# Group norm with three neighbouring channels on a partition

## The chip, the cores and the metric

The kernel runs on one NeuronCore of a Trainium2 chip. The metric is device time in microseconds from the first to the last instruction; the number compared is the median over runs. The kernel before took 2606.68 us (median of three runs, 2600.14 to 2608.02). The profiled execution was a run of its own, of 2601.2 us, with a span of 2599.5 us in the trace and a granted TensorE clock of 0.996.

The engines are called as the profile calls them: PE (TensorE, the products), PEld (its weight loads), DVE (VectorE), ACT (ScalarE), POOL (GpSimd), SP (SyncE, which issues most of the transfers).

## What is computed

Eight images of 32 x 32 positions with 384 channels pass through two layers. The first normalizes each image by groups (32 groups of 12 channels, over all positions), applies attention with six heads and relative positions, and adds the input. The second applies layer norm and causal attention over the 1024 positions, adds, and then, for five of the eight images, a feed-forward part with binarized weights and quantized activations. The part that matters here is the group norm, in front of the query, key and value products:

```python
def _gn(v, G=32, eps=1e-5):
    B_, H_, W_, C_ = v.shape
    g = v.reshape(B_, H_, W_, G, C_ // G)
    m = jnp.mean(g, axis=(1, 2, 4), keepdims=True)
    s = jnp.var(g, axis=(1, 2, 4), keepdims=True)
    return ((g - m) / jnp.sqrt(s + eps)).reshape(v.shape)

x = x + _L0_conv_ref(_gn(x), qkv_w, qkv_b, proj_w, proj_b, rel_pos_h, rel_pos_w)
# inside _L0_conv_ref:  qkv = x.reshape(b, hw, c) @ qkv_w + qkv_b
```

The mean and the variance of a group run over 12 neighbouring channels and 1024 positions.

## The kernel before

The kernel holds the image for this step transposed: channels on the 128 partitions, positions along the free dimension, so 384 channels make three blocks of 128 (`NC = 3`). The channel of partition p in block k is 128 k + p. Groups of 12 channels don't fit evenly into blocks of 128, so a group can cross from one block into the next.

```python
NC = C // P                  # 3
GROUPS_GN = 32
CG = C // GROUPS_GN          # 12

def load_T(b):
    xT = pools.image(f"gnT_{b}")
    src = img_T[b].rearrange("(k p) t -> p k t", p=P)
    for k in range(NC):
        nc.sync.dma_start(out=xT[:, k, :], in_=src[:, k, :])
    return xT

def group_norm_T(b, xT=None):
    # ... statistics of each channel: two bn_stats of 512 positions a block, one bn_aggr a block -> mv[:, k, 0:2]
    def over_groups(src, name):                  # channels -> groups, 3 products summed in PSUM
        ps = pools.o_tile(name)
        for k in range(NC):
            nc.tensor.matmul(ps[:GROUPS_GN, 0:1], to_group[:, k, :], src(k), start=(k == 0), stop=(k == NC - 1))
        return ps[:GROUPS_GN, 0:1]

    def to_channels(src, n, name):               # groups -> channels, 3 products
        ps = pools.o_tile(name)
        for k in range(NC):
            nc.tensor.matmul(ps[:, k * n : (k + 1) * n], of_group[:, ts(k, P)], src, start=True, stop=True)
        return ps[:, : NC * n].rearrange("p (k n) -> p k n", k=NC)

    nc.vector.tensor_copy(gm[:, 0:1], over_groups(lambda k: mv[:, k, 0:1], "gmean"))
    mc = to_channels(gm[:, 0:1], 1, "cmean")
    nc.vector.tensor_tensor(d, mv[:, :, 0:1], mc, ALU.subtract)
    nc.vector.tensor_tensor(d, d, d, ALU.mult)
    nc.vector.tensor_tensor(d, d, mv[:, :, 1:2], ALU.add)
    nc.vector.tensor_scalar_add(var, over_groups(lambda k: d[:, k, :], "gvar"), 1e-5)
    nc.scalar.activation(var, var, AF.Sqrt)
    nc.vector.reciprocal(gm[:, 1:2], var)
    nc.vector.tensor_copy(cs, to_channels(gm, 2, "cstat"))
    for k in range(NC):
        nc.vector.tensor_scalar(xT[:, k, :], xT[:, k, :], cs[:, k, 0:1], cs[:, k, 1:2], ALU.subtract, ALU.mult)
    return xT
```

The query and key products (`f_qk` in the profile) contract over the channels, block by block, with weights laid out in the same way (`qkv_w.rearrange("(k p) o -> p k o", p=P)`). They are the first reader of the normalized image.

The order of the stages: image 0 is loaded and normalized first, with nothing before it. Then, for each image b, layer 0 (`layer0`), and the causal attention of layer 1 (`attention1`), in the middle of which the norm of the next image is issued:

```python
for b in range(B):
    xt, more = layer0(b, gn)
    def between():
        return group_norm_T(b + 1) if b + 1 < B else None
    gn = attention1(xt, more, b, between)        # between() is called after the value products (f_v),
    add = ffn(xt, b) if b < B_FFN else None      # before the score products (f_s, L762) and f_av (L776)
```

A framework schedules the instructions of each engine. It puts the small products of the norm between the last `f_v` product and the first few `f_s` products of the attention. The kernel also holds a second path for inputs whose softmax could overflow, which a flag guards.

Of the kernel before, what the change touches and what calls it, by code (L numbers as in the profile page):

```python
# [9 lines left out]
F32 = mybir.dt.float32  # L10
F32R = mybir.dt.float32r
I32 = mybir.dt.int32
AF = mybir.ActivationFunctionType
ALU = mybir.AluOpType
# [3 lines left out]
P = 128  # L18
B, H, W, C = 8, 32, 32, 384
T = H * W  # L20
NJ = T // P
NC = C // P
# [2 lines left out]
FF = 4 * C  # L25
NM = FF // P
GROUPS_GN = 32
CG = C // GROUPS_GN
NG = 5
QB, QEPS = 128.0, 1e-5  # L30
GSB = B // NG
# [43 lines left out]
def conv_attn_hybrid(  # L75
# [19 lines left out]
    nc = tc.nc  # L95
    assert GSB == 1
    const = ctx.enter_context(tc.tile_pool(name="const", bufs=1))
# [20 lines left out]
    def load_weights(pools):  # L118

        nc.scalar.dma_start(out=bqk, in_=qkv_b[0 : 2 * C].rearrange("(m p) -> p m", p=P))  # L120
        rel = pools.page("rel")[:, : 4 * H].rearrange("p (d i) -> p d i", d=2)
        nc.vector.memset(rel, 0.0)
        for half in range(2):
            nc.scalar.dma_start(out=rel[half * HD : (half + 1) * HD, 0, : 2 * H - 1], in_=rel_hT)
            nc.scalar.dma_start(out=rel[half * HD : (half + 1) * HD, 1, : 2 * W - 1], in_=rel_wT)
        nc.scalar.dma_start(out=bv, in_=qkv_b[2 * C : 3 * C].rearrange("(m p) -> p m", p=P))
        nc.scalar.dma_start(out=b1_sb, in_=b1.rearrange("(m p) -> p m", p=P))
        src = qkv_w.rearrange("(k p) o -> p k o", p=P)
        for i in range(3):
            nc.sync.dma_start(out=wqkv_sb[:, :, ts(i, C)], in_=src[:, :, ts(i, C)])  # L130
        nc.sync.dma_start(out=wproj_sb, in_=proj_w.rearrange("(k p) o -> p k o", p=P))
        nc.sync.dma_start(out=pb, in_=proj_b.partition_broadcast(P))
        nc.sync.dma_start(out=wv_sb, in_=wv.rearrange("(k p) o -> p k o", p=P))
        nc.sync.dma_start(out=b2_sb, in_=b2.partition_broadcast(P))

        nc.scalar.mul(wqkv_sb[:, :, 0:C], wqkv_sb[:, :, 0:C], qscale)
        nc.scalar.mul(bqk[:, 0:NPAIR], bqk[:, 0:NPAIR], qscale)
        nc.scalar.mul(rel, rel, 1.0 / qscale)
        nc.scalar.copy(rel_split[:, 0], rel)
        nc.vector.tensor_tensor(rel_split[:, 1], rel, rel_split[:, 0].bitcast(F32), ALU.subtract)  # L140
# [8 lines left out]
        out=maskT, in_=maskT, compare_op=ALU.is_ge, fill=MASKED, base=0, pattern=[[1, P]], channel_multiplier=-1  # L149
# [3 lines left out]
    for i in range(2):  # L153
# [1 line left out]
    ones = const.tile([P, HD], F32, name="ones")  # L155
    nc.gpsimd.memset(ones, 1.0)

    to_group = const.tile([P, NC, GROUPS_GN], F32, name="to_group")
    nc.gpsimd.memset(to_group, 1.0 / CG)
    nc.gpsimd.affine_select(  # L160
        out=to_group, in_=to_group, compare_op=ALU.is_ge, fill=0.0,
        base=0, pattern=[[P, NC], [-CG, GROUPS_GN]], channel_multiplier=1,
    )
    nc.gpsimd.affine_select(
        out=to_group, in_=to_group, compare_op=ALU.is_ge, fill=0.0,
        base=CG - 1, pattern=[[-P, NC], [CG, GROUPS_GN]], channel_multiplier=-1,
    )
    of_group = const.tile([GROUPS_GN, C], F32, name="of_group")
    nc.gpsimd.memset(of_group, 1.0)
    nc.gpsimd.affine_select(  # L170
        out=of_group, in_=of_group, compare_op=ALU.is_ge, fill=0.0,
        base=0, pattern=[[1, C]], channel_multiplier=-CG,
    )
    nc.gpsimd.affine_select(
        out=of_group, in_=of_group, compare_op=ALU.is_ge, fill=0.0,
        base=CG - 1, pattern=[[-1, C]], channel_multiplier=CG,
    )
    unit = const.tile([P, T], F32R, name="unit")

    def make_unit():  # L180
# [112 lines left out]
    def stages(pools):  # L293
# [7 lines left out]
            engine(dst, pt[:, : n * P].rearrange("p (i q) -> p i q", i=n))  # L301

        def load_T(b):
            xT = pools.image(f"gnT_{b}")
            src = img_T[b].rearrange("(k p) t -> p k t", p=P)
            for k in range(NC):
                nc.sync.dma_start(out=xT[:, k, :], in_=src[:, k, :])
            return xT

        def group_norm_T(b, xT=None):  # L310

            xT = load_T(b) if xT is None else xT
            st = pools.small.tile([P, NC, 2, 6], F32, tag="gst", name=f"gst_{b}")
            mv = pools.small.tile([P, NC, 2], F32, tag="gmv", name=f"gmv_{b}")
            for k in range(NC):
                for half in range(2):
                    nc.vector.bn_stats(st[:, k, half, :], xT[:, k, ts(half, 512)])
                nc.vector.bn_aggr(mv[:, k, :], st[:, k, :, :].rearrange("p a s -> p (a s)"))

            def over_groups(src, name):  # L320
                ps = pools.o_tile(name)
                for k in range(NC):
                    nc.tensor.matmul(
                        ps[:GROUPS_GN, 0:1], to_group[:, k, :], src(k), start=(k == 0), stop=(k == NC - 1)
                    )
                return ps[:GROUPS_GN, 0:1]

            def to_channels(src, n, name):
                ps = pools.o_tile(name)
                for k in range(NC):  # L330
                    nc.tensor.matmul(ps[:, k * n : (k + 1) * n], of_group[:, ts(k, P)], src, start=True, stop=True)
                return ps[:, : NC * n].rearrange("p (k n) -> p k n", k=NC)

            gm = pools.small.tile([GROUPS_GN, 2], F32, tag="gm", name=f"gm_{b}")
            nc.vector.tensor_copy(gm[:, 0:1], over_groups(lambda k: mv[:, k, 0:1], "gmean"))
            mc = to_channels(gm[:, 0:1], 1, "cmean")

            d = pools.small.tile([P, NC, 1], F32, tag="gd", name=f"gd_{b}")
            nc.vector.tensor_tensor(d, mv[:, :, 0:1], mc, ALU.subtract)
            nc.vector.tensor_tensor(d, d, d, ALU.mult)  # L340
            nc.vector.tensor_tensor(d, d, mv[:, :, 1:2], ALU.add)
            var = pools.small.tile([GROUPS_GN, 1], F32, tag="gvar", name=f"gvar_{b}")
            nc.vector.tensor_scalar_add(var, over_groups(lambda k: d[:, k, :], "gvar"), 1e-5)
            nc.scalar.activation(var, var, AF.Sqrt)
            nc.vector.reciprocal(gm[:, 1:2], var)
            cs = pools.small.tile([P, NC, 2], F32, tag="gcs", name=f"gcs_{b}")
            nc.vector.tensor_copy(cs, to_channels(gm, 2, "cstat"))
            for k in range(NC):
                nc.vector.tensor_scalar(
                    xT[:, k, :], xT[:, k, :], cs[:, k, 0:1], cs[:, k, 1:2], ALU.subtract, ALU.mult  # L350
                )
            return xT

# [571 lines left out]
        def run(pools):  # L925
            gn = load_T(0)
            if pools.fast:
                load_weights(pools)
            gn = group_norm_T(0, gn)
            if pools.fast:  # L930
                make_unit()
# [25 lines left out]
    with ExitStack() as scope:  # L957
        pools = Pools(scope, tc, "f")
# [43 lines left out]
```

## Time and profile before

| what | value |
|---|---|
| median of three runs | 2606.68 us |
| span of the profiled execution | 2599.5 us |
| PE busy | 2521.0 us, 97% |
| DVE busy | 1619.4 us, 62% |
| ACT busy | 1157.0 us, 45% |
| POOL busy | 115.5 us, 4% |
| gmean and gvar records (128x32 weights, one column) | 48 each, 176 ns mean |
| cmean and cstat records (32x128 weights, one or two columns) | 48 each, 262 ns mean |
| aggregation over 12 numbers (DVE) | 24, 200 ns mean |
| normalization, 128x1024 (DVE) | 24, 809 ns mean |
| load of one block of an image, 512 KB | 24, 4.5 us median to landing |

Busy times overlap, since the engines work side by side. A product of float32 operands leaves two records of PE and two of PEld, so the 48 records of gmean are 24 products: three for each of eight images. Records of PE overlap each other[...]; the distance from start to start says what one costs in a row of products. In a line of the timeline the first number is the start, the second the duration (of all instructions merged in it), and a bracket at the end tells how long the engine was idle before it and which instruction released it. "L762" is a line of the kernel. "out<-in" are the names in the program: `f_s` is a tile of scores, `f_gmean` the PSUM tile of the group means, and so on; the leading "f_" is the fast path.

### The profile page before, as it was taken

The numbers are of one execution on the slowest core, as the hardware profiler recorded it, in microseconds if no ns is written. First come the engines' busy times: TensorE is split into PE (matmuls) and PEld (weight loads), VectorE is DVE, ScalarE is ACT, GpSimd is POOL, SyncE is SP. The second block draws the span as 40 slices with busy tenths as digits, with TensorE's granted clock in tenths as the row PEclk, the third lists the DMA queues.
The fourth block names the chain that finished last, engine by engine and source line by source line (L and its number), as shares of the span: only waits on it lengthen the run. The fifth ranks groups of instructions, "written<-read, shape, count | busy, mean of one in ns | idle before, by whom it ended". The sixth has DMA issues, their size and how long they took to land. (4 is left out here: it accounts for less than half of the span.)

```text
span 2599.5 us, 25162 instructions
## 1 busy us (share of the span) xinstructions
PE 2521.0 (97%) x9538; PEld 1508.4 (58%) x9538; DVE 1619.4 (62%) x2407; ACT 1157.0 (45%) x1513; POOL 115.5 (4%) x106
## 2 busy tenths in 40 slices
PE   7999998999999999999999999999999999999998
PEld 4555685555765556755557555576555555555554
DVE  5895468763587644786545776347864486538652
ACT  4641377421666314764127643156641264127420
POOL 1000002000001000010000100000100010001000
PEclk9999999999999999999999999999999999999999
DMA  6431106011042101150110601003200240015000
GB/s 167 147 146 61 37 1 170 1 61 37 1 117 54 49 13 37 41 130 1 61 37 1 170 1 61 6 31 91 80 25 1 67 104 1 25 39 131 1 1 26
DMA packets 148993, 144.72 MB, mean 56 GB/s; under 512 B 107264, under 2 KB 129664, under 8 KB 147328
## 3 DMA queue, kind: packets, MB, share of 16 engines
q1 hardware_dynamic: 142928, 119.36, 16.4%
q0 software_dynamic: 2880, 23.59, 2.6%
q8 instruction: 77, 1.26, 0.2%
q10 hardware_dynamic: 3056, 0.08, 0.1%
q14 instruction: 52, 0.43, 0.1%
HBM read 75.38 MB, written 42.47 MB: 45 GB/s over the span
## 5 line engine op out<-in xcount | busy, mean ns | idle before, releaser
L558 ACT ACTIVATE f_pr<-f_s 128x1024 f32<-128x1024 f32 x384 | 393.0, 1027 | 403.2 <-PE f_s L554 370.3
L567 DVE TENSOR_TENSOR f_sum<-f_sum,f_pr 128x1024 f32<-128x1024 f32 x288 | 349.0, 1244 | 147.0 <-ACT f_pr L558 145.6
L572 PE MATMUL f_av<-f_pr,f_v 128*64 128x512 f32 x1536 | 359.7, 599 | 0.0
L554 PE MATMUL f_s<-f_q,f_k 128*128 128x512 f32 x768 | 258.5, 418 | 21.8 <-ACT f_pr L558 14.9
L388 PE MATMUL f_qk<-f_gnT,wqkv_sb 128*128 128x512 f32 x576 | 261.5, 598 | 8.2 <-DVE f_k L456 5.6
L554 PE MATMUL f_s<-f_q,f_ks 128*128 128x512 f32 x768 | 245.3, 401 | 0.0
L554 PE MATMUL f_s<-f_r,unit 128*128 128x512 f32 x768 | 243.1, 398 | 0.0
L572 PEld LDWEIGHTS f_av<-f_pr,f_v 128*64 128x64 f32 x1536 | 103.2, 136 | 202.8 <-issue 195.0
L507 DVE TENSOR_TENSOR f_r<-f_near,f_r 32x1024 fp32r<-32x1024 f32 x96 | 193.7, 2017 | 29.0 <-ACT f_r L506 26.3
L554 PEld LDWEIGHTS f_s<-f_q,f_k 128*128 128x128 f32 x768 | 125.8, 189 | 137.9 <-issue 50.3
L762 PE MATMUL f_s<-f_q,f_lnT 128*128 128x512 f32 (+3 forms) x576 | 201.4, 491 | 0.0
L776 PE MATMUL f_av<-f_v,f_pr 128*128 128x385 f32 x576 | 194.5, 486 | 0.0
L388 PEld LDWEIGHTS f_qk<-f_gnT,wqkv_sb 128*128 128x128 f32 x576 | 108.0, 191 | 124.3 <-issue 114.0
L554 PEld LDWEIGHTS f_s<-f_q,f_ks 128*128 128x128 f32 x768 | 145.6, 190 | 35.9
L554 PEld LDWEIGHTS f_s<-f_r,unit 128*128 128x128 f32 x768 | 145.8, 190 | 34.8
L776 PEld LDWEIGHTS f_av<-f_v,f_pr 128*128 128x128 f32 x576 | 108.6, 190 | 78.6 <-issue 11.5
L506 ACT CAST f_r<-f_near 32x1024 fp32r<-32x1024 f32 x96 | 145.9, 1520 | 2.3
L398 PE MATMUL f_v<-wqkv_sb,f_gnT 128*128 128x384 f32 x384 | 129.4, 490 | 10.5 <-ACT f_v L512 8.3
L762 PEld LDWEIGHTS f_s<-f_q,f_lnT 128*128 128x128 f32 x576 | 100.1, 190 | 67.7 <-issue 43.5
L877 DVE TENSOR_REDUCE am<-f_h 128x1 f32<-128x1024 f32 (+2 forms) x80 | 71.6, 946 | 96.6 <-ACT f_h L870 96.6
L770 ACT ACTIVATE f_pr<-f_s 128x1024 f32<-128x1024 f32 (+3 forms) x64 | 41.7, 651 | 202.0 <-DVE f_s L767 202.0
L870 ACT ACTIVATE f_h<-f_y,b_sb 128x256 f32<-128x256 f32 x240 | 100.8, 472 | 67.0 <-PE f_y L866 67.0
(163 smaller groups left out, 3360.6 us busy)
## 6 DMA issues: line engine op xcount, KB each, us to landing
f_far<-f_far SPq DMA_DIRECT2D x48, 512.0 KB, 2.9
f_ks<-f_k SPq DMA_DIRECT2D x96, 256.0 KB, 5.1
f_gnT<-in_xT SPq DMA_DIRECT2D x24, 512.0 KB, 4.5
f_near<-f_far SPq DMA_DIRECT2D x96, 128.0 KB, 3.9
f_x<-in_x SPq DMA_DIRECT2D x32, 384.0 KB, 6.4
out_y<-f_x SPq DMA_DIRECT2D x32, 384.0 KB, 3.8
f_w1a<-w1s POOLq DMA_DIRECT2D x5, 1536.0 KB, 7.2
f_w2a<-w2s POOLq DMA_DIRECT2D x5, 1536.0 KB, 6.6
```

The costliest lines, as they stand in the source:

```text
L388: nc.tensor.matmul(ps[:, half, :], w[:, k, cols], xT[:, k, ts(half, 512)], start=(k == 0), stop=(k == NC - 1),)
L398: nc.tensor.matmul(ps[:, :C], xT[:, k, ts(j, P)], w[:, k, cols], start=(k == 0), stop=(k == NC - 1))
L506: nc.scalar.copy(dst[ts(hi, 32)], src)
L507: nc.vector.tensor_tensor(dst[ts(lo, 32)], src, dst[ts(hi, 32)].bitcast(F32), ALU.subtract)
L554: nc.tensor.matmul(sc[:, half, :], keys[:, ts(c, P)], queries[:, ts(half, 512)], start=(i == 0), stop=(i == 2))
L558: nc.scalar.activation(pr, sc.rearrange("p a n -> p (a n)"), AF.Exp)
L567: nc.vector.tensor_tensor(sums[par], prev, prs[par], ALU.add)
L572: nc.tensor.matmul(avs[half][ts(par, HD), :], v[:, c, ts(h, HD)], prs[par][:, ts(half, 512)], start=(c == 0), stop=(c == NJ - 1),)
L762: nc.tensor.matmul(sc[:, half, lo:], xT[:, c // 4, k, ts(c % 4, P)], q[:, half, k, lo:], start=(k == 0), stop=(k == NC - 1),)
L776: nc.tensor.matmul(av[:, : C + 1], prs[c][:, ts(j - c, P)], v[:, c, :], start=(c == 0), stop=(c == j))
L870: nc.scalar.activation(pairs[i][:, m, :, :], ps[:, ts(i % 2, 256)].rearrange("p (j q) -> p j q", j=2), AF.Identity, bias=b1_sb[:, m : m + 1],)
L877: nc.vector.tensor_reduce(am[:, i, n - 1 : n], pairs[i][:, cuts[n - 1] : cuts[n], :, :], AX.XYZ, ALU.max, apply_absolute_value=True)
```

## The change

The channels are laid out anew: partition p holds the three neighbouring channels 3p, 3p + 1 and 3p + 2. A group of 12 channels is then four whole partitions, and no group crosses a block. The statistics of all three channels of a partition are aggregated together; one product with a 128 x 128 matrix that holds 1/4 where two partitions belong to the same group sums over the group and spreads the sum back to its partitions in one step. A first such product gives the mean, a second the variance. The rows of the query, key and value weights are laid out in the same new order. Its purpose is to have two small products an image in place of twelve, and fewer small vector operations.

The diff, cut to its core:

```diff
-CG = C // GROUPS_GN
+NP_GN = P // GROUPS_GN
...
-        src = qkv_w.rearrange("(k p) o -> p k o", p=P)
+        src = qkv_w.rearrange("(p k) o -> p k o", k=NC)
...
-    to_group = const.tile([P, NC, GROUPS_GN], F32, name="to_group")      # memset, two affine_selects
-    of_group = const.tile([GROUPS_GN, C], F32, name="of_group")          # memset, two affine_selects
+    over_group = const.tile([P, P], F32, name="over_group")
+    nc.gpsimd.memset(over_group, 1.0 / NP_GN)
+    for low in (True, False):
+        nc.gpsimd.affine_select(...)                                     # keeps the blocks of 4 x 4
...
-            src = img_T[b].rearrange("(k p) t -> p k t", p=P)
+            src = img_T[b].rearrange("(p k) t -> p k t", k=NC)
...
-            mv = pools.small.tile([P, NC, 2], F32, tag="gmv", name=f"gmv_{b}")
+            mv = pools.small.tile([P, 2], F32, tag="gmv", name=f"gmv_{b}")
             for k in range(NC):
                 for half in range(2):
                     nc.vector.bn_stats(st[:, k, half, :], xT[:, k, ts(half, 512)])
-                nc.vector.bn_aggr(mv[:, k, :], st[:, k, :, :].rearrange("p a s -> p (a s)"))
-            ... over_groups and to_channels, gmean, cmean, gvar, cstat: 12 products, as shown above
+            nc.vector.bn_aggr(mv, st.rearrange("p k a s -> p (k a s)"))
+
+            ps = pools.o_tile(f"gmean_{b}")
+            nc.tensor.matmul(ps[:, 0:1], over_group, mv[:, 0:1], start=True, stop=True)
+            cs = pools.small.tile([P, 2], F32, tag="gcs", name=f"gcs_{b}")
+            nc.vector.tensor_copy(cs[:, 0:1], ps[:, 0:1])
+            d = pools.small.tile([P, 2], F32, tag="gd", name=f"gd_{b}")
+            nc.vector.tensor_tensor(d[:, 0:1], mv[:, 0:1], cs[:, 0:1], ALU.subtract)
+            nc.vector.scalar_tensor_tensor(d[:, 1:2], d[:, 0:1], d[:, 0:1], mv[:, 1:2], ALU.mult, ALU.add)
+            ps = pools.o_tile(f"gvar_{b}")
+            nc.tensor.matmul(ps[:, 0:1], over_group, d[:, 1:2], start=True, stop=True)
+            nc.vector.tensor_scalar_add(d[:, 0:1], ps[:, 0:1], 1e-5)
+            nc.scalar.activation(d[:, 0:1], d[:, 0:1], AF.Sqrt)
+            nc.vector.reciprocal(cs[:, 1:2], d[:, 0:1])
             for k in range(NC):
                 nc.vector.tensor_scalar(
-                    xT[:, k, :], xT[:, k, :], cs[:, k, 0:1], cs[:, k, 1:2], ALU.subtract, ALU.mult
+                    xT[:, k, :], xT[:, k, :], cs[:, 0:1], cs[:, 1:2], ALU.subtract, ALU.mult
                 )
```

The order of PE's instructions in the two programs differs in the norm alone. Before, for images 1 to 7: three gmean, one score product, three cmean, one score product, three gvar, one score product, three cstat, and the other scores. After: one gmean, two score products, one gvar, and the other scores.

More of the change, by code (lines that the diff above doesn't have):

```diff
@@ L156, in conv_attn_hybrid @@
     nc.gpsimd.memset(ones, 1.0)
-    to_group = const.tile([P, NC, GROUPS_GN], F32, name="to_group")
[L159 to L167, printed above, removed]
-    of_group = const.tile([GROUPS_GN, C], F32, name="of_group")
[L169 to L177, printed above, removed]
+    over_group = const.tile([P, P], F32, name="over_group")
+    nc.gpsimd.memset(over_group, 1.0 / NP_GN)
+    for low in (True, False):
+        nc.gpsimd.affine_select(
+            out=over_group, in_=over_group, compare_op=ALU.is_ge, fill=0.0, base=0 if low else NP_GN - 1,
+            pattern=[[-NP_GN if low else NP_GN, GROUPS_GN], [0, NP_GN]], channel_multiplier=1 if low else -1,
+        )
     unit = const.tile([P, T], F32R, name="unit")
@@ L317, in group_norm_T @@
                     nc.vector.bn_stats(st[:, k, half, :], xT[:, k, ts(half, 512)])
[L318 to L344, printed above, removed]
@@ L345, in group_norm_T @@
-            nc.vector.reciprocal(gm[:, 1:2], var)
-            cs = pools.small.tile([P, NC, 2], F32, tag="gcs", name=f"gcs_{b}")
-            nc.vector.tensor_copy(cs, to_channels(gm, 2, "cstat"))
+            nc.vector.bn_aggr(mv, st.rearrange("p k a s -> p (k a s)"))
[3 more added lines that the diff above has]
+            nc.vector.tensor_copy(cs[:, 0:1], ps[:, 0:1])
```

## The prediction

> **What bounds the kernel now.** I read the page from the top: the engine totals, then the chain that ended last. After that, because the change touches only the group norm, I read the timeline around it. From the page of the kernel before, the totals and the chain by engine:
>
> ```profile
> PE 2521.0 (97%) x9538; PEld 1508.4 (58%) x9538; DVE 1619.4 (62%) x2407; ACT 1157.0 (45%) x1513; POOL 115.5 (4%) x106
> ...
> PE 27%; ACT 1%; DMA 1%; DVE 1%; issue 0%; SPq 0%; ACTq 0%
> ```
>
> TensorE (PE) is busy 97% of the span, and the chain, which the profile follows back over the last 30% of the span, lies on PE for 27 of those 30 points. So a microsecond taken out of PE's own queue should come off the time, and a microsecond taken off another engine should not, unless PE stands waiting for it. The group norm appears in two surroundings. For image 0 it runs alone, before anything else can start. For images 1 to 7 it runs inside the attention of the image before. The timeline of PE in the last of those seven (start, duration, instruction; "x6" is six records merged):
>
> ```profile
> 2271.29 0.35 PE L323 MATMUL f_gmean<-gmv,to_group 128*32 128x1 f32 x6
> 2271.57 1.12 PE L762 MATMUL f_s<-f_q,f_lnT 128*128 128x512 f32 x2
> 2272.63 0.82 PE L331 MATMUL f_cmean<-gm,of_group 32*128 32x1 f32 x6
> 2273.38 1.12 PE L762 MATMUL f_s<-f_q,f_lnT 128*128 128x512 f32 x2
> 2274.44 0.35 PE L323 MATMUL f_gvar<-gd,to_group 128*32 128x1 f32 x6
> 2274.72 1.12 PE L762 MATMUL f_s<-f_q,f_lnT 128*128 128x512 f32 x2
> 2275.77 0.83 PE L331 MATMUL f_cstat<-gm,of_group 32*128 32x2 f32 x6
> 2276.53 0.70 PE L762 MATMUL f_s<-f_q,f_lnT 128*128 128x512 f32 x1
> ```
>
> The four small groups stand in PE's queue between score products (f_s), and no idle time is noted before any of them. PE works through this stretch without a pause, so what it spends on them is lost to the scores. One product in float32 leaves two records, so "x6" is three products. The same eight rows with the same spacing, within 0.01 us, come at 256, 605, 955, 1303, 1651, 2000 and 2271 us: seven times.
>
> For image 0 the timeline of all engines shows the norm as the path to the first real product (f_qk):
>
> ```profile
> 10.28 0.20 DVE L318 BATCH_NORM_AGGREGATE gmv<-gst 128x2 f32<-128x12 f32 x1
> ...
> 11.13 1.41 PE L331 MATMUL f_cmean<-gm,of_group 32*128 32x1 f32 x6 [0.33 <-DVE gm L335]
> 11.27 1.16 ACT L136 ACTIVATE wqkv_sb<-wqkv_sb 128x1152 f32<-128x1152 f32 x1 [3.04 <-DMA wqkv_sb<-in_qkv_w]
> 12.45 1.28 ACT L344 ACT_TABLE_LOAD   x1
> ...
> 13.70 0.14 DVE L343 TENSOR_SCALAR gvar<-f_gvar 32x1 f32<-32x1 f32 x1 [0.58 <-PE f_gvar L323]
> 13.88 0.20 ACT L344 ACTIVATE gvar<-gvar 32x1 f32<-32x1 f32 x1
> 14.11 0.15 DVE L345 RECIPROCAL gm<-gvar 32x1 f32<-32x1 f32 x1 [0.27 <-ACT gvar L344]
> 14.31 1.43 PE L331 MATMUL f_cstat<-gm,of_group 32*128 32x2 f32 x6 [0.66 <-DVE gm L345]
> 15.79 0.16 DVE L347 COPY gcs<-f_cstat 128x6 f32<-128x6 f32 x1 [1.52 <-PE f_cstat L331]
> ...
> 16.94 1.19 PE L388 MATMUL f_qk<-f_gnT,wqkv_sb 128*128 128x512 f32 x1 [1.20 <-DVE f_gnT L349]
> ```
>
> The reader is to see one serial chain, PE to DVE to ACT and back, and that ScalarE has its square root table only at 12.45 + 1.28 = 13.73 us.
>
> **What the Trainium skill says.** "TensorE: Matmul & The Clock Gate", section "LDWEIGHTS (loading the stationary operand)", says that a weight load is paid by columns, and that 32x128 weights cost what 128x128 cost. The trace agrees as far as it goes: cmean (32x128 weights) takes (2273.38 - 2272.63) / 6 = 0.125 us a record, gmean (128x32) only 0.28 / 6 = 0.047. So I size the new 128x128 product with one column as cmean. Part 1 of the same page says that PE starts at half clock and is released by a free-running window of about 3.4 us of activity. The trace agrees in kind: weight loads of the first f_qk products follow each other every 0.85 us until about 22 us, and then every 0.43. "ScalarE: Activation LUTs", section "What ACT_TABLE_LOAD costs", gives 1283 ns; the trace has 1.28 us.
>
> **The change, part by part.**
>
> *Images 1 to 7, on PE's path.* From the start of gmean to the start of the fourth score product PE needs 2276.53 - 2271.29 = 5.24 us. Three score products undisturbed take 3 x 2 x 0.43 = 2.58 us (0.43 is the spacing of records once the stretch is over, from the weight loads below). The overhead is 2.66 us. It splits into the small products (0.28 + 0.75 + 0.28 + 0.76 = 2.07, from start to next start) and three breaks: a score product followed by a small one takes 1.06 us instead of 0.86, so 3 x 0.20 = 0.60. The break shows in the timeline of weight loads (PEld), where a small group's first load starts only when the score records are done:
>
> ```profile
> 2272.62 0.74 PEld L331 LDWEIGHTS f_cmean<-gm,of_group 32*128 32x128 f32 x6 [0.76 <-DVE gm L335]
> ...
> 2277.06 0.19 PEld L762 LDWEIGHTS f_s<-f_q,f_lnT 128*128 128x128 f32 x1 [0.24 <-issue]
> 2277.49 0.19 PEld L762 LDWEIGHTS f_s<-f_q,f_lnT 128*128 128x128 f32 x1 [0.24 <-issue]
> ```
>
> After, the order of PE's instructions is gmean, two score products, gvar, the rest of the scores, and nothing else on PE moves. Two products of two records at 0.125 are 0.50, plus one break of 0.20: 0.70. Saved: 2.66 - 0.70 = 1.96 us an image, 13.7 us for seven.
>
> *Image 0, on the chain.* One aggregation over 36 numbers replaces three over 12. It still comes after the last statistics and the fold reductions, so it starts near 10.2 us. I take 0.28 us for it (177 ns for 6 numbers and 200 for 12 in the groups), ending where the old one did, at 10.5. PE is cold here (1.41 / 6 = 0.235 a record), so gmean ends near 11.05. Then copy, subtract and one fused multiply-add, 0.2 us each start to start, reach 11.65; gvar takes 0.5, the addition of epsilon 0.15, and the variance is ready at 12.3, where it was 13.84. But the table is ready only at 13.73, since ScalarE first waits for weights (to 11.27), scales them and loads the table. None of that changes. So the square root starts at about 13.75 (before: 13.88), the reciprocal ends near 14.15, and with cstat and its copy gone the normalization starts at 14.2 instead of 15.98. Saved: 1.8 us, of which 1.65 is cstat and its copy; the first half of the chain gives only 0.13, since a table load takes its place.
>
> *Off the path.* DVE loses two aggregations of 0.2 us and two of its seven small operations an image; GpSimd builds one constant instead of two. Both sit idle enough that I count nothing. Loads of the image and of the weights fetch every third row instead of neighbouring ones, in pieces of unchanged length (4 KB and 1.5 KB).
>
> Sum: 13.7 + 1.8 = 15.5 us.
>
> **Rivals.** *The saving is hidden*: PE finishes the scores earlier and then waits for something else, and the time stays near 2606. Against it: in the list of waits no f_s, L762, or f_av, L776, product waits for anyone, and the first exponential ends at 2280.36 while its reader runs at 2286.7. *A new wait for gvar*: two score products (1.9 us with the break) now separate gmean from gvar, and DVE needs its copy of f_v (to 2271.96) and three small operations, so about 2272.5, while gvar comes up at about 2273.5. One microsecond of slack; if it failed, some 0.5 us an image, 3.5 us in all, would come back. *A 128-row load is dearer*: at the 0.19 us of the f_qk weight loads four records cost 0.26 more an image, and the saving falls by 1.8 us in all. *Strided loads are slower*: for images 1 to 7 the load is issued some 30 us before the statistics (2214 against 2244.6) and lands within 6.3, so it is hidden anyway; for image 0, where the statistics wait 3.58 and 0.62 us for it, each microsecond shows, perhaps 1 to 2 us. *The cold clock*: with the first product at 15.1 instead of 16.9, the full clock may come anywhere between one window earlier and the same moment as now. In the second case the gain at the start is halved.
>
> **Range and chances.** From 2606.7, less 15.5, I get 2591. The three runs of before spread over 8 us, with one at 2600 that the profile's 2601 matches, so the median may stand a little high; I choose 2590. The rivals make the saving 9 to 18 us, and the spread of the runs adds some 4 us each way: 2582 to 2597. Faster by 2% would need 52 us, three times all that the group norm costs PE; slower by 2% would need a fault in the loads of more than 6 us an image, and these have 30 us to hide in. So within 2% is nearly certain.
>
> **What would show it.** In the changed profile: gmean to fourth score product 3.3 us instead of 5.24, seven times, with no wait noted before gvar; small products at about 0.125 us a record; the square root of image 0 right after its table load near 13.75 and the first f_qk near 15.1; the same waits for the image load. It is wrong if PE shows a wait for the variance, if idle time after the scores grows by what the norm gave up, or if the first statistics start later than 4.64 us.

## The result and the profile after

The changed kernel took 2578.73 us (median of four runs, 2577.22 to 2584.84), against 2607.35 us for the kernel before on the same occasion (four runs, 2600.14 to 2608.29): a ratio of 0.9901, with a 95% interval of 0.9877 to 0.9925. That is 28.6 us. The prediction was 2590, with 2582 to 2597 as its range, from a saving of 15.5 us; so the direction and the size within 2% were right, and the saving was larger than the range allowed. Section by section below: about 20 us of the 28.6 belong to the change, the rest to how far runs of one kernel lie apart.

From the page of the changed kernel, the totals and the chain by engine (busy us, share, instructions; shares of the span):

```profile
PE 2499.4 (97%) x9378; PEld 1495.9 (58%) x9378; DVE 1615.3 (63%) x2375; ACT 1156.5 (45%) x1513; POOL 113.8 (4%) x103
...
PE 27%; DMA 1%; ACT 1%; DVE 1%; issue 0%; ACTq 0%; SPq 0%; DVEq 0%
```

PE is still the bound. It has lost 160 records, which is ten products of two records for each of eight images, and 21.6 us of busy time, close to the 22.0 us that the span lost (2599.5 to 2577.5). The timeline of PE in the changed kernel, at the norm inside the attention of the last image but one:

```profile
2253.41 0.28 PE L310 MATMUL f_gmean<-gmv,over_group 128*128 128x1 f32 x2
2253.55 1.96 PE L735 MATMUL f_s<-f_q,f_lnT 128*128 128x512 f32 x4
2255.36 0.28 PE L317 MATMUL f_gvar<-gd,over_group 128*128 128x1 f32 x2
2255.49 2.39 PE L735 MATMUL f_s<-f_q,f_lnT 128*128 128x512 f32 x5
```

The order is the one that was forecast: gmean, two score products, gvar, scores, and no wait before gvar. But a small product is gone in 2253.55 - 2253.41 = 0.14 us: its second record starts 0.03 us behind its first, and the next score 0.11 behind that. The two scores between take 1.81 us, only 0.09 more than the 1.72 that they take alone, where a break of 0.20 was reckoned. From gmean to the fourth score product it is 2.08 us to the row with "x5", and 0.94 for the third score product in it: 3.02 us, where it was 5.24 before and 3.28 in the forecast.

The timeline of weight loads in the same stretch shows why:

```profile
2254.50 0.19 PEld L735 LDWEIGHTS f_s<-f_q,f_lnT 128*128 128x128 f32 x1 [0.24 <-issue]
2254.93 0.19 PEld L317 LDWEIGHTS f_gvar<-gd,over_group 128*128 128x128 f32 x1 [0.24 <-DVE gd L315]
2255.36 0.19 PEld L317 LDWEIGHTS f_gvar<-gd,over_group 128*128 128x128 f32 x1 [0.24 <-issue]
```

Loads go on at their 0.43 us, and the load of gvar's weights at 2254.93 runs a whole record ahead of its product at 2255.36, while the last score record is still running. In the kernel before, the first load of a small group stood at its own product's start, 2272.62 against 2272.63.

For image 0, from the timeline of all engines of the changed kernel:

```profile
10.97 0.31 DVE L307 BATCH_NORM_AGGREGATE gmv<-gst 128x2 f32<-128x36 f32 x1
...
12.07 1.16 ACT L136 ACTIVATE wqkv_sb<-wqkv_sb 128x1152 f32<-128x1152 f32 x1 [3.97 <-DMA wqkv_sb<-in_qkv_w]
...
13.25 1.28 ACT L319 ACT_TABLE_LOAD   x1
13.31 0.16 DVE L318 TENSOR_SCALAR gd<-f_gvar 128x1 f32<-128x1 f32 x1 [0.68 <-PE f_gvar L317]
14.55 0.20 ACT L319 ACTIVATE gd<-gd 128x1 f32<-128x1 f32 x1
14.78 0.16 DVE L320 RECIPROCAL gcs<-gd 128x1 f32<-128x1 f32 x1 [1.32 <-ACT gd L319]
14.98 2.26 DVE L322 TENSOR_SCALAR f_gnT<-f_gnT,gcs 128x1024 f32<-128x1024 f32 x3
...
15.94 1.19 PE L361 MATMUL f_qk<-f_gnT,wqkv_sb 128*128 128x512 f32 x1 [2.67 <-DVE f_gnT L322]
```

The variance is ready at 13.47, where 12.3 was forecast: the aggregation starts at 10.97 and not at 10.2. It holds nothing up, for the table is ready only at 14.53, and the root follows the table. The table is late because ScalarE scaled the weights from 12.07 on, 0.8 us later than before (11.27). The first real product comes at 15.94: 1.0 us earlier than before, where 1.8 was forecast.

### The profile page after: what moved, and what is told of

Same layout as the page of the kernel before. It is cut to its first block, busy times and chain, and to the rows that moved or that the text cites. A ratio compares the mean times of both kernels' runs of the same rounds, so it can differ in the third digit from the quotient of the medians.

```text
span 2577.5 us, 24797 instructions
## 1 busy us (share of the span) xinstructions
PE 2499.4 (97%) x9378; PEld 1495.9 (58%) x9378; DVE 1615.3 (63%) x2375; ACT 1156.5 (45%) x1513; POOL 113.8 (4%) x103
```

## The experiments

The expectations below speak of theories by letters. **A**: the change is worth the 16 to 20 us of the two stages above, and the rest of the 28.6 lies in stages that differ from run to run; its rival gives all 28.6 to the change. **T**: the break between a score and a small product comes from the change of tile shape (128x128 to 128x32 or 32x128); its rivals are **W**, under which the stretch keeps its length with padded weights, and **N**, under which only the number of products counts. **L**: the length of the skipped second path sets the tail. **S**: the new order of the weights' rows makes the weights land later.

To compare single traces I cut each at the same events on PE. "Ten stages" are, for images 1 to 5, the first attention and the stretch from the feed-forward part of the image before into the next query and key products; "norm stages" are the seven from gmean to the first f_av of the second attention; "rest" is the span less the ten stages. Two more columns belong to the ten stages: "extra f_x" is the time by which the forty additions to x on DVE that end the feed-forward part (f_x from f_y) take more than 0.615 us each, and "half clock" counts the stretches of 3.4 us in which the trace gives half the TensorE clock.

| trace | first f_qk | ten stages | extra f_x | half clock | norm stages | after the last product | rest |
|---|---|---|---|---|---|---|---|
| before | 16.94 | 1239.5 | 5.7 | 4 | 108.1 | 8.85 | 1360.0 |
| before, again | 19.24 | 1236.2 | 5.2 | 1 | 108.1 | 8.72 | 1362.8 |
| before, no clamp | 16.85 | 1241.7 | 0.0 | 6 | 108.1 | 9.52 | 1360.6 |
| before, full rows | 16.93 | 1236.3 | 3.4 | 3 | 104.1 | 8.99 | 1355.8 |
| four partial | 16.33 | 1245.0 | 7.9 | 6 | 100.0 | 7.58 | 1350.7 |
| after | 15.94 | 1237.8 | 5.2 | 3 | 91.8 | 7.10 | 1339.8 |
| after, again | 16.01 | 1240.4 | 6.8 | 4 | 91.8 | 7.43 | 1339.8 |
| after, third | 15.73 | 1248.9 | 10.9 | 6 | 91.8 | 7.24 | 1339.7 |
| after, no clamp | 16.35 | 1243.1 | 0.0 | 7 | 91.8 | 7.42 | 1341.0 |
| after, early root table | 15.05 | 1247.8 | 12.5 | 5 | 91.8 | 7.38 | 1339.2 |
| after, long second path | 16.11 | 1238.6 | 6.9 | 2 | 91.8 | 7.23 | 1340.1 |
| after, weights old | 15.08 | 1237.8 | 6.2 | 2 | 91.8 | 7.47 | 1338.8 |
| after, image old | 16.36 | 1241.9 | 8.3 | 3 | 91.8 | 7.45 | 1341.1 |
| after, both old | 17.07 | 1241.0 | 7.6 | 3 | 91.8 | 7.58 | 1341.5 |

### Both kernels again

No edit: the kernel before and the changed kernel, run again beside the kernel before.

> The kernel before, once more, for a second trace and for its own spread. The traces so far give the norm 2.3 us in each of seven images (16.2 us), 0.6 us more in the stage ahead of it, and 1.7 us in image 0: some 18 us, while the medians differ by 28.6. Theory A: the other 10 us are a draw. In the five feed-forward images the final additions on VectorE (f_x from f_y) run beside GpSimd's clamp of f_y, and one of them sometimes takes 1 to 3 us instead of 0.6; the longest draw differs from run to run. Then this trace has the same norm stages as before to 0.05 us, its feed-forward stages differ from the first trace's by up to 2.5 us each, and its times lie at 2600 to 2609. Theory B: the old layout costs more in every run elsewhere (addresses, loads). Then the stages that are longer than in the changed kernel are the same ones in both traces of before.

> The changed kernel, once more. Both theories: norm stages of 13.1 us from gmean to the second attention's first value product, times of 2576 to 2586. Theory A (the draw of VectorE beside GpSimd's clamp): the feed-forward stages that are long are others than in the first trace. Theory B (a lasting gain elsewhere): they are the same, and shorter than in both traces of before. The first statistics of the third block of image 0 started at 9.22 us here against 8.59 before: if the strided load causes it, it stays near 9.2; if it is a draw, it does not.

Measured: before again 2602.20 us (14 runs, 2596.53 to 2607.69), ratio 1.0001 (0.9992 to 1.0011); after again 2581.56 (6 runs, 2581.10 to 2587.78) against 2601.62 (27 runs of before, 2597.57 to 2610.68), ratio 0.9927 (0.9914 to 0.9940). The difference is 20.1 us. In the table the norm stages repeat to 0.1 us and the rest of the three traces of the unedited changed kernel to 0.1, while the ten stages differ by up to 11 us between them. So the first medians lay some 5 us high before and 3 us low after, by chance, and theory A holds: a difference of 20, not 28.6. Two details were not as expected. The runs of before reached down to 2596.5 and not 2600. And the long feed-forward stretch was no other one: it is the fifth in all three traces of the unedited changed kernel (113.0, 113.2 and 114.6 us, against 111.0 and 111.7 in the two of before). Since it is longer there and not shorter, this is no gain elsewhere. The first statistics of the third block of image 0 started at 8.86 us and not at 9.22, so that delay was a draw.

### The clamp on GpSimd taken away

The feed-forward part clamps its output on GpSimd. The same edit to both kernels; it leaves the clamp of the quantized output out.

```diff
-for j in range(NJ):
-    nc.gpsimd.tensor_scalar(y[:, j, :], y[:, j, :], up, low, ALU.min, ALU.max)
```

> The kernel before without GpSimd's clamp of the feed-forward output (the clamp is left out: values at the quantization limits keep up to 1e-5 of it). Theory A (additions on VectorE stretched by the clamp beside them): no addition of f_x takes over 0.8 us, the feed-forward stages of the five images agree within 0.3 us, the spread of the runs falls from 8 us to some 3, and the time falls by 3 to 10 us to about 2597 to 2604. Theory B: the spread and the stages stay as they are.

> The changed kernel without the same clamp. Theory A: 18 us below the kernel before without the clamp (16 to 20), since only the norm and the start of image 0 differ. Theory B (a lasting gain of some 10 us elsewhere): 26 to 29 us below it.

Measured: before without it 2603.97 us (13 runs, 2600.89 to 2606.06), ratio 1.0002 (0.9992 to 1.0012); after without it 2585.48 (6 runs, 2581.80 to 2587.59), ratio 0.9932 (0.9920 to 0.9944). The two differ by 18.5 us. The addition to x that follows the clamp, from the view of tile f_x on DVE (count: shortest/median/longest ns), in the kernel before:

```profile
L919 DVE SCALAR_TENSOR_TENSOR f_x<-f_y,qs,f_x x40: 605/617/2547, 403.1 to 1806.2; 128x384 f32<-128x384 f32 x40
```

The same row for the kernel before without the clamp:

```profile
L916 DVE SCALAR_TENSOR_TENSOR f_x<-f_y,qs,f_x x40: 610/613/621, 396.4 to 1804.4; 128x384 f32<-128x384 f32 x40
```

The longest of 40 is 2.5 us beside the clamp, and 0.62 without it. In the changed kernel the longest is 3.5 us (x40: 605/615/3515), and 0.62 without the clamp. The timeline of GpSimd in the kernel before shows a run of eight clamps:

```profile
401.37 5.78 POOL L915 TENSOR_SCALAR f_y<-f_y,qu,ql 128x384 f32<-128x384 f32 x8 [7.15 <-issue]
```

And this is DVE's timeline of the same kernel at the same moment:

```profile
403.13 3.48 DVE L919 SCALAR_TENSOR_TENSOR f_x<-f_y,qs,f_x 128x384 f32<-128x384 f32 x2
406.63 1.52 DVE L456 SCALAR_TENSOR_TENSOR f_k<-f_qk,bqk,f_k 64x512 fp32r<-64x512 f32 x2
```

Two additions of 0.62 take 3.48 us while GpSimd clamps, and DVE's next work, the evacuation of f_k that PE waits for, comes after them. The Trainium skill, "SBUF — State Buffer", section "SBUF: two separate sides", says that a VectorE operation with two SBUF inputs and a GpSimd operation that reads SBUF lock each other out for a whole instruction; the pair above agrees in kind. In size it goes further: the pair lost 2.2 us, and one clamp takes 0.65.

Without the clamp the feed-forward stretches agree in both traces: 111.3, 111.3, 111.6, 111.2, 111.3 and 111.3, 111.3, 111.6, 111.3, 111.3 us, where the traces of the unedited changed kernel spread from 110.5 to 114.6. So the clamp is shown to be what scatters those five, and the stretches follow the extra time of their additions: with the clamp and at full clock they run from 110.5 us with 0.3 us of extra time to 113.5 with 3.0. The spread of the runs of before fell as well, from 13 us (27 runs) to 5 (13 runs). The expectation that the median would fall by 3 to 10 us was missed: it stayed (2604 against 2602). The quiet feed-forward stretches of the kernel before add up to 556.7 us, as much as the scattered ones (556.8 and 556.4); why they are no shorter isn't settled.

The first-attention stages still vary, from 136.6 to 138.1 us in these two. What goes with that is the granted clock. The busy times by window (length, then the busy time of each engine; the third number from the end is the granted clock) of two of these stages in the changed kernel:

```profile
411.97:547.80 135.83, 132.13 (x544) 74.60 (x544) 100.01 (x87) 77.72 (x77) 8.59 (x3) 1.00 0.24 66
1102.10:1238.90 136.80, 133.48 (x545) 75.49 (x545) 100.02 (x87) 77.77 (x77) 9.28 (x3) 0.99 0.24 65
```

Of the 70 such stages in all fourteen traces, the 27 in which the clock stayed full took 135.9 us on the mean, the 40 with one stretch of half clock 136.9, and the three with two such stretches 137.9. Both traces without the clamp have one or two in each of these stages. Less some 1.1 us for each stretch of half clock and less the extra time of the additions, the ten stages of the twelve traces with the clamp would take 1229.2 to 1231.4 us, where they took 1236.2 to 1248.9. So these two make nearly all of their scatter. What brings the half clock on isn't shown.

### The old layout with weights padded to 128 rows

```diff
-    of_group = const.tile([GROUPS_GN, C], F32, name="of_group")
+    gm = const.tile([P, 2], F32, name="gm")
+    nc.gpsimd.memset(gm, 0.0)
+    of_group = const.tile([P, C], F32, name="of_group")      # rows 32 to 127 are zero
...
-    nc.vector.tensor_copy(gm[:, 0:1], over_groups(lambda k: mv[:, k, 0:1], "gmean"))
+    nc.vector.tensor_copy(gm[:GROUPS_GN, 0:1], over_groups(lambda k: mv[:, k, 0:1], "gmean"))
...
```

All twelve products stay; cmean and cstat now have 128x128 weights.

> The kernel before, still with twelve products in the old layout, but the matrix that spreads the groups (of_group) has 128 rows, 96 of them zero, and so has gm: cmean and cstat become 128x128 products like the scores around them; gmean and gvar keep their 32 columns. Theory T (a change of the tile's shape in the array): a weight load of another shape than the running product's is not started under it. Then cmean's and cstat's first loads now start about 0.43 us ahead of their products, gmean's and gvar's still do not, a record of cmean still takes 0.11 us, and the way from gmean to the fourth score product falls from 5.24 to about 4.7 us. Theory W (the wait for VectorE's result holds the load back): nothing changes, 5.24 us. Time: 4 us less by T, the same by W, both within the spread.

Measured: from gmean to the fourth score product 4.69 us (before 5.24), the norm stages 104.1 us, 4.0 less than before. The medians don't resolve so little: 2598.34 us (12 runs), ratio 0.9993 (0.9980 to 1.0005). The timeline of weight loads of this kernel:

```profile
2264.60 0.30 PEld L763 LDWEIGHTS f_s<-f_q,f_lnT 128*128 128x128 f32 x2
2265.13 0.19 PEld L333 LDWEIGHTS f_cmean<-gm,of_group 128*128 128x128 f32 x1 [0.24 <-DVE gm L336]
2265.56 0.64 PEld L333 LDWEIGHTS f_cmean<-gm,of_group 128*128 128x128 f32 x5 [0.24 <-issue]
...
2266.12 0.30 PEld L763 LDWEIGHTS f_s<-f_q,f_lnT 128*128 128x128 f32 x2
2267.18 0.26 PEld L325 LDWEIGHTS f_gvar<-gd,to_group 128*32 128x32 f32 x6 [0.76 <-DVE gd L342]
```

The padded load of cmean starts at 2265.13, one record ahead of its product at 2265.56. The load of gvar, still 128x32 wide, starts only at 2267.18, with its own product. The bracket names DVE, but DVE's row says that the operand was there 0.31 us earlier, at 2266.87:

```profile
2266.71 0.16 DVE L342 TENSOR_TENSOR gd<-gd,gmv 128x3 f32<-128x3 f32 x1
```

So gvar's load stood until the score records were through. One kernel shows both cases side by side. Theory T holds, and W falls: cmean waits for a result of DVE too, and its load ran ahead all the same. The load of cstat runs 0.24 us ahead and not 0.43, since its operand comes only then; its product isn't later for it. Of the two groups padded, each saves some 0.27 us: 0.1 in the score ahead (1.06 to 0.96) and 0.17 in the group (0.755 to 0.587, from its start to the next score). The score record after a small product still takes 0.51 us from start to start, against 0.53 before and 0.43 undisturbed: that cost is not the shape's.

### The new layout with four products of changed shape

```diff
-    over_group = const.tile([P, P], F32, name="over_group")          # 1/4 within a group
+    to_group = const.tile([P, GROUPS_GN], F32, name="to_group")      # 1/4 within a group
+    of_group = const.tile([GROUPS_GN, P], F32, name="of_group")      # 1 within a group
...
-    nc.tensor.matmul(ps[:, 0:1], over_group, mv[:, 0:1], start=True, stop=True)
+    nc.tensor.matmul(ps[:GROUPS_GN, 0:1], to_group, mv[:, 0:1], start=True, stop=True)     # gmean, copied to gm
+    nc.tensor.matmul(ps2[:, 0:1], of_group, gm[:, 0:1], start=True, stop=True)             # cmean
```

(gvar and cstat likewise.)

> The changed kernel's layout, but with four products an image in place of two: to 32 groups (128x32), back to 128 partitions (32x128), twice. Theory T (shape changes cost by themselves): from gmean to the fourth score product 2.57 for the scores, 0.30 + 0.61 for the products and 0.6 for the shape changes, 4.1 us in all; changed kernel 3.02, before 5.24. Theory N (only the number of records counts, 24 before, 4 after, 8 here): 3.46 us. Time by T some 8 to 9 us above the changed kernel (7 x 1.1, and 0.7 to 1.5 in image 0), by N some 4.

Measured: 2593.68 us (10 runs, 2587.74 to 2599.67), ratio 0.9971 (0.9958 to 0.9984). The timeline of PE of this kernel:

```profile
2269.89 0.22 PE L323 MATMUL f_gmean<-gmv,to_group 128*32 128x1 f32 x2
2270.04 1.12 PE L754 MATMUL f_s<-f_q,f_lnT 128*128 128x512 f32 x2
2271.09 0.38 PE L326 MATMUL f_cmean<-gm,of_group 32*128 32x1 f32 x2
2271.40 1.13 PE L754 MATMUL f_s<-f_q,f_lnT 128*128 128x512 f32 x2
2272.46 0.22 PE L332 MATMUL f_gvar<-gd,to_group 128*32 128x1 f32 x2
2272.61 1.12 PE L754 MATMUL f_s<-f_q,f_lnT 128*128 128x512 f32 x2
2273.66 0.38 PE L338 MATMUL f_cstat<-gm,of_group 32*128 32x2 f32 x2
```

From gmean to the fourth score product (2273.97) it is 4.09 us, as T had it, and not the 3.46 of N. The distance from a score to the next small product is 2271.09 - 2270.04 = 1.05 us, the same 0.2 over 0.86 as with three times as many small products before. So the norm stages fall by 8.1 us (108.1 to 100.0) from having four products in place of twelve, and by another 8.2 (to 91.8) from having two, both of the scores' own shape. The median lies 10 to 12 us above those of the changed kernel (2581.6 to 2583.3), where T had 8 to 9, and "rest" 10.9 above.

### The root's table loaded early

In the changed kernel, ahead of the scaling of the weights:

```diff
+        early = const.tile([P, 1], F32, name="early_sqrt")
+        nc.scalar.activation(early, ones[:, 0:1], AF.Sqrt)
```

> The changed kernel, with a square root of a constant ahead of the scaling of the weights in image 0, so that ScalarE loads the square root's table while it waits for the weights. If the table load after the scaling is what the norm of image 0 ends on, the root starts right after the scaling or the variance instead of 2.48 us after the scaling's start, 1.0 to 1.1 us earlier, and the first query product starts near 15.0 us (changed kernel: 15.94, 16.01). If the norm ends on something else, it starts where it did. The time falls by some 1 us, less than the spread.

Measured: 2581.97 us (6 runs, 2577.64 to 2588.70), ratio 0.9924 (0.9905 to 0.9942). The timeline of ScalarE of this kernel:

```profile
8.13 1.28 ACT L137 ACT_TABLE_LOAD   x1
...
12.60 1.16 ACT L138 ACTIVATE wqkv_sb<-wqkv_sb 128x1152 f32<-128x1152 f32 x1 [2.98 <-DMA wqkv_sb<-in_qkv_w]
13.67 0.19 ACT L321 ACTIVATE gd<-gd 128x1 f32<-128x1 f32 x1
```

The table is loaded in idle time, no second load follows the scaling, the root runs at 13.67, 1.07 us after the start of the scaling instead of 2.48 and right behind the variance (written at 13.54), and the first f_qk comes at 15.05 instead of 15.94. So the table was the bound of image 0 in the changed kernel. Its 0.9 us is in the trace and can't be seen in medians that spread over 11 us.

### A longer second path, and a third trace

The tail after the last product fell from 8.85 to 7.10 us, which was in no step of the prediction. The second path, which the flag skips, shrank with the change as well. This edit of the changed kernel lengthens only that path:

```diff
+            if not pools.fast:
+                # ten more small products and four more copies for each norm
```

> The changed kernel; only the second path, which these inputs skip, is made longer again: ten more small products and four more copies in each of its eight norms, so that TensorE's part of it is as long as in the kernel before (12,792 instructions as scheduled, 12,712 in the changed kernel). In the traces so far the time from the last product to the end of the span is 8.7 to 9.5 us with the old norm and 7.1 to 7.6 with the new one, and TensorE's branch over the second path takes 4.2 to 4.5 us against 3.4 to 3.5. Theory L (what has to be skipped sets the branch's time): the branch takes 4.2 us or more and the tail is near 9 us, so the time rises by some 1.6 us. Theory M (something else in the program, such as where its code lies): the branch stays near 3.5 and the tail near 7.4.

> The changed kernel a third time, for its spread. The span without the ten stages that draw (query products and feed-forward, and first attention, of images 1 to 5) was 1339.8 us in both of its traces and 1360.0 and 1362.8 us in those of before. If the change is worth 20 us and the rest is a draw, that sum is 1339 to 1341 again, the ten stages add up to anything from 1236 to 1248, and the median lies 18 to 22 us below before.

Measured: 2582.57 us (5 runs), ratio 0.9933 (0.9920 to 0.9945), with a tail of 7.23 us; the changed kernel itself 2583.30 (6 runs, 2577.35 to 2590.39) against 2601.45 (11 runs), ratio 0.9927 (0.9914 to 0.9940), with 7.24. Theory L falls: with the longer path PE's branch over it takes 3.4 us. It takes 3.4 to 3.9 us in all ten traces of the new layout and 4.2 to 4.5 in all four of the old. The record of DMA packets has a companion to this: one packet of 16 KB of instructions moves during the branch, in 1.0 to 1.3 us with the new layout and 1.9 to 2.0 with the old, and in every trace the branch ends 1.3 to 1.5 us after it has landed. So the branch seems to wait for instructions; why they come later in the old program stays open, and so does the rest of the 1.75 us, some 0.7, which passes after the branch.

### The rows of the weights, of the image, and both in the old order

Each edits the changed kernel, and computes another function at the same cost, since channels no longer meet their weights, or, with both in the old order, a group no longer gathers its own channels.

```diff
-        src = qkv_w.rearrange("(p k) o -> p k o", k=NC)          # weights_old, both_old
+        src = qkv_w.rearrange("(k p) o -> p k o", p=P)
-            src = img_T[b].rearrange("(p k) t -> p k t", k=NC)   # image_old, both_old
+            src = img_T[b].rearrange("(k p) t -> p k t", p=P)
```

> The changed kernel with the rows of the query, key and value weights in the old order (it leaves the weights unmatched to the channels, so it computes another function at the same cost). In image 0 the scaling of the weights started at 11.05, 11.17, 11.27 and once 13.70 us with the old norm and at 11.64 to 12.60 us in seven traces with the new one, and the first of the three weight transfers takes 0.68 us to issue instead of 0.38. Theory S (the new order of the weights' rows): issue 0.38 us again, scaling near 11.2, root near 13.7, first query product near 15.1. Theory X (the image's rows, loaded just before): issue 0.68 or the scaling near 12.1, first query product near 16.0.

> The changed kernel with the image's rows in the old order (groups then gather the wrong channels; the cost of the norm is the same). Theory S (order of the weights' rows): issue of the first weight transfer 0.68 us, scaling near 12.1 us, first query product near 16.0. Theory X (order of the image's rows): 0.38 us or scaling near 11.2, first query product near 15.1.

> The changed kernel with both loads in the old order (another function at the same cost). Both theories: issue 0.38 us, scaling near 11.2 us, root right after the table near 13.7, first query product near 15.1, some 0.9 us earlier than in the changed kernel. If the scaling stays near 12.1, neither order of rows is the cause.

Measured, one run each: 2578.28, 2584.66 and 2584.28 us. Two rows of the timeline matter: the issue of the three weight transfers, and the scaling that waits for them. With the weights alone in the old order:

```profile
6.77 1.45 SPq L130 DMA_DIRECT2D wqkv_sb<-in_qkv_w  x3
...
11.21 1.16 ACT L136 ACTIVATE wqkv_sb<-wqkv_sb 128x1152 f32<-128x1152 f32 x1 [3.14 <-DMA wqkv_sb<-in_qkv_w]
```

The same rows with the image alone in the old order:

```profile
6.77 2.00 SPq L130 DMA_DIRECT2D wqkv_sb<-in_qkv_w  x3
...
12.49 1.16 ACT L136 ACTIVATE wqkv_sb<-wqkv_sb 128x1152 f32<-128x1152 f32 x1 [4.36 <-DMA wqkv_sb<-in_qkv_w]
```

And with both in the old order:

```profile
6.93 1.44 SPq L130 DMA_DIRECT2D wqkv_sb<-in_qkv_w  x3
...
13.20 1.16 ACT L136 ACTIVATE wqkv_sb<-wqkv_sb 128x1152 f32<-128x1152 f32 x1 [4.89 <-DMA wqkv_sb<-in_qkv_w]
```

The issue follows the order of the weights' rows in every trace, 1.45 us old and 2.00 new. The start of the scaling follows it in the first two (and the first f_qk: 15.08 and 16.36 us), as S expected, but not in the third, where 11.2 was expected. Over all traces it starts at 11.05 to 11.27 in four with the old order and at 13.20 and 13.70 in two, and at 11.64 to 12.60 in eight with the new. So 0.55 us of issue is shown; that the weights usually land about 1 us later with the new order is likely; why they sometimes land at 13.2 is open. The image's order shows no such effect (image_old's 12.49 lies within those eight).

The early table alone and the old order of the weights alone bring the first f_qk to 15.05 and 15.08 us. Both together were not run; since the variance is ready at 13.47 to 13.54 and the root ran at 13.67 and 13.69, little more could come of it (an estimate from these traces).

## Why the prediction was right, and where it was wrong

**What bounds the kernel, and the rivals: right.** PE's own queue carried the saving through to the end; no wait took its place. The variance path has slack, though less than the microsecond that was reckoned: the operand of gvar is written at 2254.69 us, and its product starts at 2255.36. The loads of later images stayed hidden. The first statistics began at 4.71 us, 0.07 later than the 4.64 named as a sign of being wrong, with no effect on the root.

**Images 1 to 7: right in kind, too small.** The step that failed is "Two products of two records at 0.125 are 0.50, plus one break of 0.20: 0.70". The overhead measured 3.02 - 2.58 = 0.44: two products of 0.14 make 0.28 and not 0.50, and the 0.08 or 0.09 by which the record after each runs longer make 0.17 in place of the break. The price of 0.125 a record was the larger miss: the load of a small product had run ahead, so its first record lasted only 0.03 us. The prediction had read rightly that "a small group's first load starts only when the score records are done", and took it for a trait of small products. The padded kernel and the one of four products show that it belongs to the change of shape. That is 0.26 us an image, 1.8 in all. Moreover, two smaller costs of the old shape were not in the sum: 0.09 us ahead of gmean and 0.10 in the score behind cstat, 1.3 us for seven. Together 13.7 + 1.8 + 1.3 = 16.8; the traces give 108.1 - 91.8 = 16.3 in the norm stages and 0.65 ahead of them.

**Image 0: the bound was named rightly, its time was not.** The aggregation cost about what was reckoned (0.31 us against 0.28) but began 0.8 us later, and from its end to the variance it took 2.2 us and not 1.8; neither showed, for the table was indeed what held the root back. The step that failed is "None of that changes": ScalarE waited for weights to 12.07 and not 11.27, so the root came at 14.55 and not 13.75, and 1.8 us became 1.0. The prediction looked for slower strided loads in the image alone. The full clock came earlier all the same (20.17 us against about 22.07), and the rest of image 0 ran 0.6 us shorter; that makes 1.6.

**What the sum didn't hold.** The tail after the last product gave 1.75 us, its cause open. Norm stages 16.3, ahead of them 0.65, image 0 1.6, tail 1.75: 20.3 us, and "rest" fell by 1360.0 - 1339.8 = 20.2. The two later comparisons of medians give 20.1 and 18.2. The ten stages could take back a little: their mean is 1237.3 us in three traces of the old layout (both of before and the padded one) and 1241.8 in eight of the new with two products and the clamp in place (1236.2 to 1239.5 against 1237.8 to 1248.9). A single addition of more than 3 us stands in eight of the nine traces of the new layout with the clamp (these eight and four partial, which took 1245.0) and in none of the three of the old. That points to the layout, but so few traces, each with such a scatter, don't settle it.

**The base and the range.** The last failure is in the choice "I choose 2590". The text saw that the first median might stand high and took 1 us off; the later runs of before have medians of 2600.8 to 2602.2, some 5 below it. The changed kernel's first four runs fell low by about 3. With a saving of 20 and the later medians the changed kernel stands at 2581.6 to 2583.3, at the edge of the range; the first measurement lay 3 us outside.

## What to carry to other kernels

Between products of one shape, keep small products in that shape, by padding rows with zeros if need be: on a full PE queue the switch to a tile of 32 rows and back cost some 0.27 us, and a small product of the scores' own shape 0.14. Padding of columns was not run; at 0.11 instead of 0.03 us a record, a group of six records would lose more by it than the switch costs (an estimate from the records of cmean and gmean). When a chain is shortened, look for the next bound in every engine that it meets, and ask of each transfer that the change lays out anew whether someone stands waiting for it at the start. Before a saving of half a per cent is judged by medians, cut traces at the same events: stages that repeat to 0.1 us told here what runs spread over 12 us could not.

## What was not expected of the hardware

- A 128x128 load runs a whole record (0.43 us) ahead under a running 128x128 product, but a 128x32 or 32x128 load between such products waits for the records to be done. For a group of 32x128 products the switch there and back cost some 0.27 us, gone with padding. The Trainium skill, "TensorE: Matmul & The Clock Gate", Part 3, section "The mechanism", says that loads are pulled ahead of running products if they go to another row group or to the background buffer; the traces agree for whole tiles and add that the change of shape stops it.
- A small product with 128x128 weights and one column cost 0.14 us from start to next start, and 0.08 to 0.09 in the next product.
- Additions of 0.62 us on VectorE beside GpSimd's clamp took up to 3.5 us in the changed kernel, though one clamp takes 0.65 us.
- A stretch of 3.4 us at half the granted clock made a first-attention stage of 136 us some 1.1 us longer.
- Three weight transfers of 576 KB took 1.45 us to issue with rows 128 apart on a partition, and 2.00 us with neighbouring rows.
- PE's branch over the skipped path took 4.2 to 4.5 us in one layout and 3.4 to 3.9 in the other, with a longer path 3.4, and ended 1.3 to 1.5 us after a packet of instructions had landed.
